# A four-layer graph network on one core: 64-wide products in pairs, a merged first message round, and a sorting network written with another instruction

## The chip, the core and the metric

The kernel runs on one core of one Trainium2 chip. The metric is device time in microseconds (us) for one execution, over all 16 batches; the median of three runs before the change is 3176.69 us (3176.14 to 3177.83). A profiled execution, from which every duration below is read, is a separate run with the profiler on.

A core has five engines with a queue each, which they work through in order: PE (TensorE, matmuls), DVE (VectorE), ACT (ScalarE), POOL (GpSimd; here it only issues gathers) and SP (SyncE, which issues DMAs). ACT and POOL issue DMAs too.

## The reference

`x` is 16 x 1024 x 64, `adj` 16 x 1024 x 1024 with about 17 nonzero entries per row, the diagonal among them. Four layers, each ending in a layernorm over the 64 channels:

```python
# layer 0
x = layernorm(x + adj @ (x @ W0) + b0)
# layer 1: quantiles over the kept neighbours of each node
adj_ = where(eye, 1, adj);  nb = (adj_ > 0) & ~eye;  m = nb.sum(-1)
rank = cumsum(nb, -1) - 1
skip = where(m > 10, (m + 1) // 2, 1)
removed = nb & (skip > 1)[..., None] & ((rank + 1) % skip[..., None] == 0)
adj_d = where(removed | removed.T, 0, adj_)
sv = sort over the kept neighbours' rows of x, channel by channel
agg = 0.25*q(0.25) + 0.5*q(0.5) + 0.25*q(0.75)      # interpolated from sv
x = layernorm(x + (relu((x + agg) @ W1 + b1) @ W2 + b2) * nodemask)
# layer 2: h = x @ We, then three message rounds
for i in range(3):
    h = relu(adj @ (h @ Wl[i] + bl[i]))
x = layernorm(x + (h @ Wp + bp) * nodemask)
# layer 3
t = adj @ x
x = layernorm(x + where(t > 0.5, 1, 0))
```

## The kernel before

**Tiles.** A batch's 1024 nodes are eight tiles (`T` = 8) of 128 (`P`); C = 64 channels, H = 128 hidden, R = 66 the pitch of a gathered row, `HALF` = 512 nodes, `NH` = 2 halves, `TH` = 4 tiles in a half. PE writes into PSUM banks of 128 partitions by 512 floats. "Node form" has nodes on the partitions, "channel form" has channels there.

**Stages of a batch.** Each is a Python generator that issues a few instructions and yields their planned length.

- `words_of` loads 128 rows of the adjacency at a time (SP, 512 KB), transposes them on PE (L439), copies them on ACT (L441), compares with zero on DVE (`nb`, L526 and L527), packs the neighbour bits into words by matmuls (L536), and feeds layer 0: `Layer0.feed` (L459 to L468) makes eight products of 64 output rows for each tile (L464). `Layer0.end` transposes `x` into the lower 64 partitions of `ax` (L478), so that one product with `w0_sb` (128 x 64, the weight above a centred identity) adds the node itself.
- `front` and `listing` work out which neighbours stay and list them (DVE: MAX8 at L707, `scalar_tensor_tensor` at L694 and L710, permutation at L646) and write a table of `x` to DRAM.
- `gathered` has POOL fetch one listed neighbour's row for each of the 128 nodes of a tile per indirect DMA (L815): 129 of them per batch. They land in the tile `g` (tag "x", four buffers).
- `masked` marks the end of each list (DVE L862, ACT L868).
- `quantiles` sorts the gathered rows: a network of minima and maxima on DVE, all at L906, 228 `tensor_tensor` instructions per batch, 3648 in all. Each takes two boxes of SBUF and writes a third, `count` by `run` slots of 64 columns; `box` builds them with a stride of 66. Neighbouring instructions depend on each other often.
- `summed` weighs the sorted rows (ACT L932) and adds them up on PE (L936).
- `back` takes the sums back to node order (`to_nodes`, one-hot matmuls at L979, closing products at L985), then w1 (L1172), residual (L1141, L1147) and layernorm; layer 2: `to_channels` (transposes L367, copies L369), We (L1185), and three rounds of message (bias L324, weight L1196, copy L1199) and product with the adjacency (L1207, relu L1210), then a residual; layer 3: `aggregate` (L372 to L381, products at L377), transposes at L1219, threshold L1222, layernorm, store.

**What is 64 wide.** The products of `feed` (L464), `aggregate` (L377), `to_nodes` (L979, L985) and the transposes of `to_channels` have 64 output rows; they fill partitions 0 to 63 of a bank, one bank for each half of the nodes, and one ACT copy of 64 x 512 for each bank. Channel-form tiles (`chan`) are 64 x 1024.

**Order.** All batches are recorded in one order, worked out in Python ahead of time: a heap of generators by planned time (L1233 to L1271). `LENGTHS` are the planned lengths of the five sort groups of a batch (192.06 us together); `WORDS`, `LISTS` and `BACK` (152.6, 133.2 and 178 us) are how long the other stages should last, and each is spread over that time by the factor `WORDS / WORDS_STEPS` and so on, where the `_STEPS` are what a stage's own yields add up to. What is recorded is what each engine's queue runs, in that order. So stages of neighbouring batches share the engines: while batch b is sorted, POOL gathers for a later group, the rows of batch b+1 are read and packed, and the back of batch b-1 runs. For batch 0's head there is nothing to sort yet; behind the last sort only the last batch's back is left. A spare branch behind it (`general`, which shares `feed`, `to_channels` and `back`) handles batches whose lists overflow; no instruction of it is in the trace.

Of the kernel before, what the change touches and what calls it, by code (L numbers as in the profile page):

```python
# [53 lines left out]
WORDS_STEPS, LISTS_STEPS, BACK_STEPS = 82.0, 74.0, 181.0  # L54
# [94 lines left out]
def network(n):  # L149
    return [tuple(map(int, op.split(","))) for op in NETS[n].split(";")]  # L150


@with_exitstack
def kernel(
# [126 lines left out]
    nc.scalar.dma_start(w0_sb[:C, :], w0)  # L281
    nc.vector.tensor_copy(w0_sb[C:, :], ident[C:, C:])
    w1_sb = load("w1_sb", [C, H], w1)
    b1_sb = load("b1_sb", [H, 1], b1.unsqueeze(1))
    w2_sb = load("w2_sb", [H, C], w2)
    we_sb = load("we_sb", [C, H], we)
# [11 lines left out]
    for v, n in ((w0_sb, 2 * C), (w2_sb, H), (wp_sb, H)):  # L298
        centred(v, n)
# [21 lines left out]

    def add_bias(bank, first, n, times):

        nc.tensor.matmul(bank[:, :times * n], ones16,  # L324
                         bias16[:, first:first + n].unsqueeze(1).to_broadcast([S, times, n]),
                         start=True, stop=False)
# [4 lines left out]
    mask_f = const.tile([B * T, P], F32, name="mask_f")  # L331
# [10 lines left out]
    def psum_mm():  # L342
        return psum("mm", 2)
# [17 lines left out]

    def to_channels(dst, src):

        for h in range(NH):
            pt = psum_mm()
            for i in range(TH):
                nc.tensor.transpose(pt[:C, i * P:(i + 1) * P], src[:, h * TH + i, :], ident)  # L367
            yield 1.5
            nc.scalar.copy(dst[:, h * HALF:(h + 1) * HALF], pt[:C, :])  # L369
            yield 1.0  # L370

    def aggregate(dst, adjT, src, bank):  # L372

        for h in range(NH):
            pa = bank()
            for m in range(T):
                nc.tensor.matmul(pa[:C, :], src[:, m, :], adjT[:, h * TH:(h + 1) * TH, m, :],  # L377
                                 start=(m == 0), stop=(m == T - 1))
                yield 1.3
            nc.scalar.copy(dst[:, h * HALF:(h + 1) * HALF], pa[:C, :])  # L380
            yield 0.7  # L381
# [38 lines left out]
    def load_x(b):  # L420
        xt = act.tile([P, T + 1, C], F32, tag="x", name="xt")
        nc.vector.memset(xt[:, 0, :], 0.0)
        nc.sync.dma_start(xt[:, 1:, :], one(x, b).rearrange("o (t p) c -> p (o t) c", p=P))
        return xt
# [27 lines left out]
    class Layer0:  # L452
# [6 lines left out]
        def feed(self, t, at):  # L459
            if t % TH == 0:  # L460
                self.bank = psum_ax()
            cols = slice((t % TH) * P, (t % TH + 1) * P)
            for m in range(T):
                nc.tensor.matmul(self.bank[:C, cols], self.xt[:, m + 1, :], at[:, m, :],  # L464
                                 start=(m == 0), stop=(m == T - 1))
            yield 2.4
            if t % TH == TH - 1:
                h = t // TH  # L468
                nc.scalar.copy(self.ax[:C, h * HALF:(h + 1) * HALF], self.bank[:C, :])
                yield 0.7  # L470

        def end(self, y):
            for h in range(NH):
                pt = psum_tp()
                for i in range(TH):

                    two = self.xt[:, h * TH + i:h * TH + i + 2, :].rearrange("p t c -> p (t c)")
                    nc.tensor.transpose(pt[:, i * P:(i + 1) * P], two, ident)  # L478
                yield 1.0
                nc.scalar.copy(self.ax[C:, h * HALF:(h + 1) * HALF], pt[C:, :])  # L480
                yield 0.7
            pz = psum_ax()
            add_bias(pz, 0, C, T)
            for t in range(T):
                nc.tensor.matmul(pz[:, t * C:(t + 1) * C], self.ax[:, t * P:(t + 1) * P], w0_sb,
                                 start=False, stop=(t == T - 1))
                if t % 2:
                    yield 0.7
            yield 1.0
            yield from layernorm(nodes(pz), y, "0")  # L490
# [400 lines left out]
    def quantiles(st, g):  # L891
        tiles, n, lo, kw = group(g)
        nt = len(tiles)
        while ("hat", g) not in st:
            yield 0.5
        bufs = st["g", g], srt.tile([P, KMAX * R], F32, tag="y", name="s", bufs=2)

        def box(buf, first, run, step, count):
            v = buf[:, first * nt * R:]
            dims = [[step * nt * R, count]] if count > 1 else []  # L900
            dims += [[R, run * nt]] if run * nt > 1 else []
            return bass.AP(tensor=v.tensor, offset=v.offset,
                           ap=[list(v.ap[0])] + dims + [[1, C]])

        for mode, a, b, d, run, sa, sb, sd, count in network(n):
            nc.vector.tensor_tensor(box(bufs[mode >> 1 & 1], d, run, sd, count),  # L906
                                    box(bufs[mode >> 3], a, run, sa, count),
                                    box(bufs[mode >> 2 & 1], b, run, sb, count),
                                    ALU.max if mode & 1 else ALU.min)
            yield (nt * count * run * C + 151) / 960  # L910
        w = tmp.tile([P, nt, kw], F32, tag="w", name="w")
        nc.vector.tensor_reduce(w, st["hat", g].rearrange("p t s k -> p t k s"), AX.X, ALU.add)  # L912
        yield 0.2
        st["sorted", g] = bufs, w
# [40 lines left out]
    def to_nodes(dst, st):  # L955
# [11 lines left out]
        banks = [psum_mm() for _ in range(NH)]  # L967
        for s in range(T):
# [8 lines left out]
            for h, bank in enumerate(banks):  # L977
                for i in range(S):
                    nc.tensor.matmul(bank[:C, :], pieces[:, i, s, :],  # L979
# [3 lines left out]
        for h, bank in enumerate(banks):  # L983
            for i in range(TH):
                nc.tensor.matmul(bank[:C, i * P:(i + 1) * P], st["x1"][:, h * TH + i, :], ident,  # L985
                                 start=False, stop=(i == TH - 1))
            yield 1.2
            nc.scalar.copy(dst[:, h * HALF:(h + 1) * HALF], bank[:C, :])
# [31 lines left out]
    def general(b):  # L1020
# [47 lines left out]
        xT = act.tile([C, N], F32, tag="chan", name="x1T")  # L1068
        run(to_channels(xT, st["x1"]))
        xrow = dram.tile([C, N], F32, tag="xrow", name="xrow", bufs=1)  # L1070
        nc.sync.dma_start(xrow, xT)
# [50 lines left out]
    def back(st):  # L1122
# [33 lines left out]
        def chan(name):  # L1156
            return act.tile([C, N], F32, tag="chan", name=name)
# [11 lines left out]
        for h in range(NH):  # L1169
            cols = slice(h * HALF, (h + 1) * HALF)  # L1170
            ph = psum_mm()
            nc.tensor.matmul(ph, w1_sb, oT[:, cols], start=True, stop=True)  # L1172
# [6 lines left out]
        x2T = chan("x2T")  # L1179
        yield from to_channels(x2T, x2)  # L1180
        hT = act.tile([H, N], F32, tag="hT", name="h0T")
        for h in range(NH):
            cols = slice(h * HALF, (h + 1) * HALF)
            ph = psum_mm()
            nc.tensor.matmul(ph, we_sb, x2T[:, cols], start=True, stop=True)  # L1185
            yield 1.3
            nc.scalar.copy(hT[:, cols], ph)
            yield 0.7
        for l in range(NL):
# [26 lines left out]
        yield from aggregate(tT, adjT, x3, psum_mm)  # L1216
        pt = psum_mm()
        for t in range(T):
            nc.tensor.transpose(pt[:, t * C:(t + 1) * C], tT[:, t * P:(t + 1) * P], ident[:C, :C])  # L1219
# [96 lines left out]
```

## Time and profile before

| | |
|---|---|
| median of three runs | 3176.69 us |
| span of the profiled execution | 4328.2 us |
| granted TensorE clock, mean | 0.764 of full speed |
| first gather starts | 96.0 us |
| sort instructions (L906) | 266.8 us to 4195.2 us, 3648 of them, 1974.6 us busy |
| last instruction ends | 4328.2 us |
| gathers (L815) | 2064, 2158.4 us busy |

The profiled execution is 1151.5 us longer than the median of the runs. Its time goes in periods of some 251 us, one for each batch, and a stretch of each has nearly idle engines. A group's "busy" is the sum of its instructions' durations; "idle before" is how long its engine stood before them, with what released it. A window's row gives, for each engine, busy time and the number of instructions, then the granted clock.

### The profile page before, as it was taken

To read this page: it belongs to the slowest core of one execution; us is meant where nothing else is said; L and a number is where in the kernel's file an instruction comes from. 1 tells how busy PE (TensorE), PEld (TensorE's weight loads), DVE (VectorE), ACT (ScalarE), POOL (GpSimd) and SP (SyncE) were. 2 spreads that over 40 slices of the span, in tenths; PEclk is the share of its full clock that TensorE was granted. 3 is DMA by queue.
4 is the path that set the end of the run, shared out by engine and by line. 5 is a ranking of instruction groups with operands and counts; after the bars stand their busy time and mean duration, and the time that the engine had idled before them with its cause. 6 is when DMAs were issued, how large, how long until landed. Compare 5 with 4: busy or idle time off the path is not lost.

```text
span 4328.2 us, 46055 instructions
## 1 busy us (share of the span) xinstructions
PE 2647.8 (61%) x13765; PEld 1635.7 (38%) x13766; DVE 2822.0 (65%) x6935; ACT 1914.0 (44%) x6153; POOL 2160.8 (50%) x2078
## 2 busy tenths in 40 slices
PE   6034285675848567584755758476575848456478
PEld 5023152443525244352533435253343525233243
DVE  6058383865849486594857668485766859476671
ACT  2034352634536264453535455363545536253641
POOL 1715626455454645546465464546545554645600
PEclk8566597787969778796877879687787969768688
DMA  3212121322222132222213222231322222111210
GB/s 107 42 50 70 34 67 37 104 54 78 73 71 84 40 101 56 78 77 74 77 39 90 64 83 76 65 84 40 100 60 79 78 80 71 39 57 24 62 43 3
DMA packets 169056, 282.54 MB, mean 65 GB/s; under 512 B 99485, under 2 KB 102112, under 8 KB 166880
## 3 DMA queue, kind: packets, MB, share of 16 engines
q1 hardware_dynamic: 67584, 142.01, 9.9%
q0 software_dynamic: 66048, 69.88, 9.1%
q10 hardware_dynamic: 35168, 67.62, 4.1%
q8 instruction: 114, 1.87, 0.2%
q14 instruction: 142, 1.16, 0.1%
HBM read 204.33 MB, written 71.44 MB: 64 GB/s over the span
## 4 chain that ended last, share of the span: by engine, by line
another core or an unknown queue 28%; DVE 25%; PE 23%; ACT 16%; issue 7%; DMA 0%; ACTq 0%; DVEq 0%
DVE g L906 7%; PE mm L1207 7%; DVE s L906 7%; ACT g L868 6%; ACT ones_at L974 3%; PE ax L464 3%; ACT ones_at L975 2%; PE tp L439 2%; PE mm L377 2%; PE pa L936 2%; PE mm L1196 2%; ACT g L932 1%; PE mm L1141 1%; DVE top L707 1%
## 5 line engine op out<-in xcount | busy, mean ns | idle before, releaser
L815 POOL DMA_INDIRECT g<-table,idx x1952 | 2045.4, 1048 | 1919.7 <-PE pa L936 666.8
L1207 PE MATMUL mm<-adjB,msg 128*128 128x512 f32 x1536 | 769.6, 621 | 109.1 <-issue 82.4
L936 PE MATMUL pa<-g,ident 128*128 128x128 f32 (+1 forms) x1600 | 376.0, 360 | 430.1 <-ACT g L932 300.5
L868 ACT ACTIVATE g<-g,bias 128x64 f32<-128x64 f32 (+9 forms) x2272 | 596.8, 341 | 47.9 <-DVE bias L864 29.2
L906 DVE TENSOR_TENSOR s<-g 128x256 f32<-128x256 f32 (+9 forms) x944 | 531.3, 588 | 64.5 <-ACT g L868 55.5
L936 PEld LDWEIGHTS pa<-g,ident 128*128 128x128 f32 x1600 | 312.3, 248 | 574.0 <-ACT g L932 347.1
L906 DVE TENSOR_TENSOR g<-s 128x256 f32<-128x256 f32 (+8 forms) x864 | 473.4, 573 | 9.0 <-DVE s L906 3.0
L932 ACT ACTIVATE g<-g,w 128x64 f32<-128x64 f32 x1552 | 397.8, 341 | 17.2 <-DVE w L912 13.6
L1207 PEld LDWEIGHTS mm<-adjB,msg 128*128 128x128 f32 x1536 | 268.7, 197 | 301.1 <-issue 270.7
L1147 DVE TENSOR_TENSOR u<-mm,mb 128x512 f32<-128x512 f32 x32 | 22.1, 691 | 463.1 <-remote 313.5
L464 PE MATMUL ax<-at,xt 128*64 128x128 f32 x1920 | 284.5, 310 | 17.4 <-issue 17.4
L377 PE MATMUL mm<-adjB,x 128*64 128x512 f32 x512 | 272.6, 666 | 36.3 <-issue 31.3
L979 PE MATMUL mm<-ones_at,pieces 128*64 128x512 bf16 x768 | 213.0, 420 | 119.0 <-ACT ones_at L975 77.1
L464 PEld LDWEIGHTS ax<-at,xt 128*64 128x64 f32 x1920 | 250.2, 158 | 81.2 <-issue 79.1
L439 PE MATMUL tp<-ident,arow 128*128 128x128 f32 x1024 | 181.7, 309 | 156.2 <-remote 66.4
L399 DVE TENSOR_REDUCE ln_v<-sq 128x8 f32<-128x512 f32 x64 | 43.6, 681 | 296.4 <-issue 156.8
L439 PEld LDWEIGHTS tp<-ident,arow 128*128 128x128 f32 x1024 | 140.9, 162 | 205.1 <-issue 131.7
L441 ACT COPY at<-tp 128x512 f32<-128x512 f32 x240 | 139.0, 580 | 177.2 <-remote 122.3
L906 DVE TENSOR_TENSOR g<-g,s 128x256 f32<-128x256 f32 (+5 forms) x432 | 199.1, 464 | 15.1 <-remote 5.0
L906 DVE TENSOR_TENSOR g<-g 128x256 f32<-128x256 f32 (+8 forms) x304 | 200.7, 660 | 11.2 <-remote 4.0
L1219 PE MATMUL mm<-ident,tT 64*128 64x64 f32 x128 | 25.7, 295 | 293.9 <-ACT tT L380 207.4
L1210 ACT ACTIVATE hlT<-mm 128x512 f32<-128x512 f32 x96 | 57.4, 598 | 296.4 <-PE mm L1207 123.7
(225 smaller groups left out, 4361.9 us busy)
## 6 DMA issues: line engine op xcount, KB each, us to landing
arow<-in_adj_dram SPq DMA_DIRECT2D x128, 512.0 KB
adjd<-at ACTq DMA_DIRECT2D x120, 512.0 KB
adjB<-adjd SPq DMA_DIRECT2D x15, 4096.0 KB
g<-table,idx POOLq DMA_INDIRECT x1952
table<-xc ACTq DMA_DIRECT2D x16, 264.0 KB
xt<-in_x_dram SPq DMA_DIRECT2D x16, 256.0 KB
out_dram<-y SPq DMA_DIRECT2D x16, 256.0 KB
stage<-table,packed POOLq DMA_INDIRECT x112
```

What stands on the lines that cost most here:

```text
L377: nc.tensor.matmul(pa[:C, :], src[:, m, :], adjT[:, h * TH:(h + 1) * TH, m, :], start=(m == 0), stop=(m == T - 1))
L439: nc.tensor.transpose(pt[:, i * P:(i + 1) * P], a[:, j * P:(j + 1) * P], ident)
L441: nc.scalar.copy(at[:, h * TH:(h + 1) * TH, :], pt.rearrange("p (i n) -> p i n", n=P))
L464: nc.tensor.matmul(self.bank[:C, cols], self.xt[:, m + 1, :], at[:, m, :], start=(m == 0), stop=(m == T - 1))
L815: nc.gpsimd.indirect_dma_start(out=dst, out_offset=None, in_=st["table"], in_offset=bass.IndirectOffsetOnAxis(ap=index, axis=0))
L868: nc.scalar.activation(v, v, AF.Identity, bias=bias[:m, i, k:k + 1])
L906: nc.vector.tensor_tensor(box(bufs[mode >> 1 & 1], d, run, sd, count), box(bufs[mode >> 3], a, run, sa, count), box(bufs[mode >> 2 & 1], b ...
L932: nc.scalar.activation(slots(g, bufs[0], lo + r, lo + r + 1)[:, i, 0, :C], slots(g, bufs[at[r]], lo + r, lo + r + 1)[:, i, 0, :C], AF.Iden ...
L936: nc.tensor.matmul(pa[:, :(e - k) * nt * C], ident, rows_.rearrange("p (k c) -> p k c", c=R)[:, :, :C], start=(j == 0), stop=(j == len(run ...
L974: nc.scalar.activation(ones_at, iota, AF.Abs, bias=st["minus"][:, s:s + 1])
L979: nc.tensor.matmul(bank[:C, :], pieces[:, i, s, :], ones_at[:, h * HALF:(h + 1) * HALF], start=(s == 0 and i == 0), stop=False)
L1207: nc.tensor.matmul(pg, msg[:, m, :], adjT[:, h * TH:(h + 1) * TH, m, :], start=(m == 0), stop=(m == T - 1))
```

## The change

It has four parts.

1. **Pairs.** `rows_of(bank, h)` is partitions 0 to 63 or 64 to 127 of a bank. `feed`, `aggregate`, `to_nodes` and `to_channels` write two products of 64 rows into the two halves of one bank, in turn, and ACT copies one 128 x 512 block where it copied two of 64 x 512. In `feed` the even neighbour tiles go to one half and the odd to the other, and the product with `w0_sb` (now the weight twice, one above the other) adds the halves; the node itself comes by a product of its own (`xT`, `self_sb`), eight more small matmuls per batch. Channel-form tiles are 128 x 512. The transposes of `to_channels` become matmuls with the identity, those at the end of layer 3 go from eight of 64 rows to four of 128, those of `Layer0.end` from eight to four.
2. **The merged first round.** Layer 2's embedding and first message weight become one 64 x 128 weight `wel_sb`, worked out once at the start: We, less its mean over the 64 inputs, times Wl[0], plus bl[0]/64 in every row. As `x2` comes out of a layernorm and so sums to zero over the channels, the product of `x2 + 1` with it equals the message with its bias. So the first round is: add one to `x2` (ACT), one paired `aggregate`, two products with `wel_sb`, relu. `to_channels(x2)`, the two products with We, two biases, 16 instructions of L1196 and one of the three rounds of L1207 are gone.
3. **Minimum and maximum.** `tensor_tensor(min or max)` becomes `scalar_tensor_tensor` (times 1.0, then min or max). Its boxes have at most two free dimensions, so where a box has more than one run, `widths` lets it run over all 66 columns of a slot.
4. **Counts.** `WORDS_STEPS` goes from 82 to 74 and `BACK_STEPS` from 181 to 149; the planned lengths of the stages stay.

```diff
-WORDS_STEPS, LISTS_STEPS, BACK_STEPS = 82.0, 74.0, 181.0
+WORDS_STEPS, LISTS_STEPS, BACK_STEPS = 74.0, 74.0, 149.0
...
+def widths(n, nt, narrow, full):
...
+    read, found = set(), []
+    for mode, a, b, d, run, sa, sb, sd, count in reversed(network(n)):
+        out = places(mode >> 1 & 1, d, run, sd, count)
+        wide = bool(out & read) or (count > 1 and run * nt > 1)
+        read -= out
+        if wide:
+            read |= places(mode >> 3, a, run, sa, count) | places(mode >> 2 & 1, b, run, sb, count)
+        found.append(full if wide else narrow)
+    return found[::-1]
...
+    weT = act.tile([H, C], F32, tag="x3", name="weT")
+    pe = ps.tile([P, HALF], F32, tag="mm", name="pe", bufs=2)
+    nc.tensor.transpose(pe[:, :C], we_sb, ident[:C, :C])
+    nc.vector.tensor_copy(weT, pe[:, :C])
+    centred(weT, H)
...
+    for h in range(2):
+        half = slice(h * C, (h + 1) * C)
+        nc.tensor.matmul(pe[half, :H], share16[:, half], bias16[:, 3 * C:3 * C + H],
+                         start=True, stop=False)
+        nc.tensor.matmul(pe[half, :H], weT, wl_sb[:, 0, :], start=False, stop=True)
+    nc.vector.tensor_copy(wel_sb, pe[:, :H])
...
+    def rows_of(t, h):
+        return t[h * C:(h + 1) * C]
+
     def to_channels(dst, src):
...
+        pt = psum_mm()
+        for i in range(TH):
+            for h in range(NH):
+                nc.tensor.matmul(rows_of(pt, h)[:, i * P:(i + 1) * P], src[:, h * TH + i, :], ident,
+                                 start=True, stop=True)
+        yield 1.5
+        nc.scalar.copy(dst, pt)
+        yield 1.0
+
+    def aggregate(dst, adjT, src, bank, tiles):
+
+        pa = bank()
+        for m in range(T):
+            for h in range(NH):
+                nc.tensor.matmul(rows_of(pa, h), src[:, m, :], adjT[:, tiles[h], m, :],
                                  start=(m == 0), stop=(m == T - 1))
-                yield 1.3
-            nc.scalar.copy(dst[:, h * HALF:(h + 1) * HALF], pa[:C, :])
-            yield 0.7
+            yield 1.3
+        nc.scalar.copy(dst, pa)
+        yield 0.7
...
             for m in range(T):
-                nc.tensor.matmul(self.bank[:C, cols], self.xt[:, m + 1, :], at[:, m, :],
-                                 start=(m == 0), stop=(m == T - 1))
-            yield 2.4
+                nc.tensor.matmul(rows_of(self.bank, m % 2)[:, cols], self.xt[:, m, :], at[:, m, :],
+                                 start=(m < 2), stop=(m >= T - 2))
+            yield 1.6
...
+                nc.tensor.matmul(pzt, self.ax[:, t * P:(t + 1) * P], w0_sb, start=False, stop=False)
+                nc.tensor.matmul(pzt, xT[:, t // 2 * P:(t // 2 + 1) * P], self_sb[:, t % 2],
                                  start=False, stop=(t == T - 1))
...
-        for mode, a, b, d, run, sa, sb, sd, count in network(n):
-            nc.vector.tensor_tensor(box(bufs[mode >> 1 & 1], d, run, sd, count),
-                                    box(bufs[mode >> 3], a, run, sa, count),
-                                    box(bufs[mode >> 2 & 1], b, run, sb, count),
-                                    ALU.max if mode & 1 else ALU.min)
-            yield (nt * count * run * C + 151) / 960
...
+        for (mode, a, b, d, run, sa, sb, sd, count), width in zip(network(n), widths(n, nt, C, R)):
+            nc.vector.scalar_tensor_tensor(box(bufs[mode >> 1 & 1], d, run, sd, count, width),
+                                           box(bufs[mode >> 3], a, run, sa, count, width), 1.0,
+                                           box(bufs[mode >> 2 & 1], b, run, sb, count, width),
+                                           op0=ALU.mult, op1=ALU.max if mode & 1 else ALU.min)
+            yield (nt * count * run * width + 151) / 960
...
             yield 1.9
-            for h, bank in enumerate(banks):
-                for i in range(S):
-                    nc.tensor.matmul(bank[:C, :], pieces[:, i, s, :],
+            for i in range(S):
+                for h in range(NH):
+                    nc.tensor.matmul(rows_of(bank, h), pieces[:, i, s, :],
                                      ones_at[:, h * HALF:(h + 1) * HALF],
                                      start=(s == 0 and i == 0), stop=False)
...
-        x2T = chan("x2T")
-        yield from to_channels(x2T, x2)
+        x2p = act.tile([P, T, C], F32, tag="msg", name="x2p")
+        nc.scalar.activation(x2p, x2, AF.Identity, bias=ones)
+        yield 1.0
+        gT = chan("gT")
+        yield from aggregate(gT, adjT, x2p, psum_mm,
+                             [slice(h * TH, (h + 1) * TH) for h in range(NH)])
         hT = act.tile([H, N], F32, tag="hT", name="h0T")
         for h in range(NH):
-            cols = slice(h * HALF, (h + 1) * HALF)
             ph = psum_mm()
-            nc.tensor.matmul(ph, we_sb, x2T[:, cols], start=True, stop=True)
+            nc.tensor.matmul(ph, rows_of(wel_sb, h), rows_of(gT, h), start=True, stop=True)
             yield 1.3
-            nc.scalar.copy(hT[:, cols], ph)
+            nc.scalar.activation(hT[:, h * HALF:(h + 1) * HALF], ph, AF.Relu)
             yield 0.7
-        for l in range(NL):
+        for l in range(1, NL):
...
-        yield from aggregate(tT, adjT, x3, psum_mm)
+        yield from aggregate(tT, adjT, x3, psum_mm, [slice(h, T, NH) for h in range(NH)])
         pt = psum_mm()
-        for t in range(T):
-            nc.tensor.transpose(pt[:, t * C:(t + 1) * C], tT[:, t * P:(t + 1) * P], ident[:C, :C])
+        for i in range(TH):
+            nc.tensor.transpose(pt[:, i * P:(i + 1) * P], tT[:, i * P:(i + 1) * P], ident)
```

## The prediction

> **What bounds the kernel now.** I read the page's top and its chain of waits first.
>
> ```profile
> span 4328.2 us, 46055 instructions
> ...
> PE 2647.8 (61%) x13765; PEld 1635.7 (38%) x13766; DVE 2822.0 (65%) x6935; ACT 1914.0 (44%) x6153; POOL 2160.8 (50%) x2078
> ...
> another core or an unknown queue 28%; DVE 25%; PE 23%; ACT 16%; issue 7%; DMA 0%; ACTq 0%; DVEq 0%
> ```
>
> No engine is full, and 28% of the chain, 1212 us, has no releaser in the trace. The span lies 1151 us above the runs' median of 3176.7, so nearly all of this belongs to the profiled execution alone: without the 1212 us it would last 3116, 2% under the median. Where that time sits, the windows show (columns: length; busy us and instructions of PE, PEld, DVE, ACT, POOL; granted clock; DMA share; GB/s):
>
> ```profile
> 2140.00:2150.00 10.00, 10.00 (x67) 6.53 (x67) 9.66 (x29) 5.70 (x19) 0.00 (x0) 1.00 0.30 107
> 2160.00:2170.00 10.00, 10.00 (x59) 6.39 (x58) 9.79 (x23) 5.98 (x20) 7.87 (x8) 1.00 0.20 38
> 2200.00:2210.00 10.00, 0.00 (x0) 0.00 (x0) 0.00 (x0) 1.58 (x8) 7.57 (x8) 0.50 0.16 27
> ```
>
> In the third only gathers run; such stretches are the profiler's. In the others DVE is busy 9.7 of 10 us. PE shows 10.00, but its ends are modelled: 2647.8 us at the mean clock of 0.764 is 2023 at full clock, 126 per batch of 181. So in the steady part DVE sets the end. Between the first sort (266.8) and the last (ends 4195.2) its instructions and the gaps under 1 us between them take 2727.3 + 105.7 = 2833 us, 177.1 per batch. The head up to the first sort is 147 us without the profiler's share: the first gather starts at 96.0, the 24 of the first group take 1.35 each, landing and masking the rest. The tail behind the last sort is 133 us and holds no gather. 147 + 2833 + 133 = 3113; the median is 64 more, 4.0 us of DVE waiting per batch. Waits of DVE in one period:
>
> ```profile
> DVE u L1147 <- remote: 32.4, 1, 32.4
> ...
> DVE u L1147 <- PE mm L1141: 6.1, 1, 6.1
> DVE cand L694 <- ACT hat L887: 2.1, 1, 2.1
> DVE s L906 <- ACT g L868: 2.1, 1, 2.1
> ```
>
> The first is the profiler's; the others, 10.3 together, are of the size wanted.
>
> **POOL is nearly level with DVE.** A gather's length depends on what DVE does (start, length, engine; the DVE row is from the same moment):
>
> ```profile
> 2101.28 1.15 POOL L815 DMA_INDIRECT g<-table,idx  x1 [0.30 <-issue]
> ...
> 2107.74 0.94 POOL L815 DMA_INDIRECT g<-table,idx  x1 [0.30 <-issue]
> ```
>
> ```profile
> 2108.20 0.55 DVE L710 SCALAR_TENSOR_TENSOR kw<-kw,top 128x320 f32<-128x320 f32 x1
> ```
>
> Sorting all 2064 gathers by the DVE operation that overlaps them most: idle DVE 946 ns (751 gathers), `tensor_tensor` of L906 1118 (998), `scalar_tensor_tensor` of L710 946 (81) and, with two whole tensors, of L694 947 by its median (10, mean 1060), reduction of L399 945 (13). Beside a DVE over 90% busy the mean is 1110. With 0.302 to the next, 2064 x 1.41 = 2914 us; plus 97 before the first gather and 212 behind the last, 3223, already above 3177. So POOL has no room, and data for the sorts can be late.
>
> **Part 3, the sorting instructions.** Price of one:
>
> ```profile
> L1147 DVE TENSOR_TENSOR u<-mm,mb 128x512 f32<-128x512 f32 x32 | 22.1, 691 | 463.1 <-remote 313.5
> ```
>
> ```profile
> L1222 DVE SCALAR_TENSOR_TENSOR u<-mm,x x16: 680/692/692, 767.3 to 4316.6; 128x512 f32<-128x512 f32 x16
> ```
>
> (The second row has minimum, median, maximum.) 512 elements cost 691 ns by the one and 692 by the other; I take no difference. Upper bound: 320 elements in L710 take 552 against 486 for a sum of that size, but that form reads a scalar per partition, ours a constant; for 8 elements the gap to a dependent instruction is 193 against 187, so 6 ns on 3648 is 22 us. Lower bound zero: no row shows it cheaper. Wider boxes: summing `count` x `run` x tiles x width over the networks of a batch, 84,736 elements become 87,314, 2,578 more; at the 0.96 per ns that L906 keeps (256: 0.42 us, 512: 0.69), 2.69 us per batch, 43 us in all. The recorded order has 82 more sort instructions waiting for the one before; after a sort instruction the next one starts 0.187 us past its elements' time when it waits for it and 0.069 when it doesn't, so each costs 0.118: 10 us. DVE sum: +53 (to +75), all on the bound engine, hidden by nothing.
>
> What it gives: with L906 acting like L694 and L710, a slot of POOL goes from 1.41 to 1.26 us, 2064 x 0.15 = 310 us of room; POOL needs 97 + 2600 + 212 = 2909 and no longer meets DVE. I let the waits fall from 4.0 to 1.0 us per batch: -48 us; bounds 0 and -64. One quarter stays because L1147 waits for PE and L694 for ACT, whatever POOL does.
>
> A rule speaks against this: the Trainium skill ("SBUF — State Buffer", Who interferes with whom) says that a DVE instruction with two SBUF inputs contends with a GpSimd instruction that reads SBUF. By it both forms, with two tensors in SBUF, would hold the gathers up alike, and the relief would be nothing. L694 has two SBUF tensors as well, and the median of its gathers, 947 ns, speaks against the rule for this form; ten are few.
>
> **Part 1, pairs.** At full clock a product of 512 columns in float32 is two instructions of 0.43 us, 128 or 64 wide alike. No row shows two 64-wide products on the two halves of a bank, so one pair costs between one product (side by side) and two (one after the other). Per batch, side by side saves 6.9 in `aggregate` (32 x 0.43 = 13.8 halved), 7 in `feed` (13.9), 5 in `to_nodes` (48 instructions x 0.22), and with part 2 the replacement of a round of 13.8 by 6.9 and the lost L1185, L1196 and L367: 29 us in all; one after the other 3.5. In the steady part either lies under DVE (126 of 181 us), and counts only as an earlier L1147. Eight small products more in layer 0 (0.1 each) are as covered. ACT loses 4.6 us per batch, of 1914 / 16 = 120, also covered. The bare stretch is the tail:
>
> ```profile
> 4243.57 15.17 PE L1207 MATMUL mm<-adjB,msg 128*128 128x512 f32 x32
> ```
>
> ```profile
> 4298.87 16.55 PE L377 MATMUL mm<-adjB,x 128*64 128x512 f32 x32 [4.79 <-DVE x L411]
> ```
>
> The stretch from x2 to the first hidden state, 4233.0 to 4259.4, is 26.4 us; a paired aggregate of 7.6 to 8.3, two copies and two products make 12 to 14: -13. L377 halves: -8. The 15.2 us of to-nodes (PE there 13.1, ACT between): -4; copies and closing products: -2. Sum -27 side by side; one after the other -8, since only the We, message and copy steps go. The halves write different partitions and depend on nothing of each other, so I take side by side.
>
> **Part 2** adds set-up. In the recorded order all of DVE's constants, with the copies of weT and `wel_sb` that wait for PE, now stand ahead of batch 0's first `nb`, which started at 14.09; behind it wait the bits, the lists and the first gather: +4 to +7. Feeding batch 0 (64.4 - 49.28 = 15 us of PE for its eight tiles) halves, some of it on that path: -3. The 24 first gathers at 0.15 less could give -4, but sorts don't run there yet, so nothing. Head +2 (-4 to +7).
>
> No DMA is added where the kernel runs: SP's order grows by one, the store at L1071 in the spare branch, which the trace shows not taken; POOL's stays as it is. The steps keep their places in SP's and POOL's order. Nothing for that.
>
> **Part 4** issues nothing. Fewer steps over the same 178 us stretch each, so L1147's first instance comes some 8 us of plan later; its row waits 6.1 for PE, and later placement can only shorten that. If instead the back ran late, the next adjB load behind it would: bounds 0 and +1 per batch, inside the 4.0.
>
> **Sum:** 147 + 2 head, 2833 + 53 steady, 133 - 27 tail, 16 waits: 3157. Against 3176.7: +2 +53 -27 -48 = -20.
>
> **Rivals.**
>
> *The boxes cost more than POOL gives (ends slower).* Place: L906 on DVE. The waits belong to PE and ACT (L1147, L694, L868 rows above), or the relief fails as by the rule; then they stay 4.0. 3176.7 + 2 + 53 - 27 = 3205. It decides where less than (53 + 2 - 27) / 16 = 1.75 us of wait per batch goes away. For it: all DVE waits in that period name PE or ACT, none a gather. Against: 3223 of POOL demand.
>
> *POOL was the only bound.* Then all 64 go, and the first gathers gain 4: 3177 + 2 + 53 - 27 - 64 - 4 = 3137; should part of the 105.7 us of small gaps also be late data (a quarter, say), 3111. For it: 3223 against DVE's 3113. Against: DVE 9.7 of 10.
>
> *Pairs run one after the other.* Tail -8: 3157 + 19 = 3176, no change. For it: nothing in the trace has such a pair. Against: nothing either.
>
> **How the numbers follow.** Forecast 0.44, slower rival 0.24, POOL alone 0.18, serial pairs 0.14. A measurement of this kernel tells 0.2% from no change: 3170.3 to 3183.0. Faster: 0.38 of the forecast, all 0.18, 0.03 of the serial case: 0.59. Same: 0.05 + 0.07 = 0.12. Slower: 0.01 + 0.04 + 0.24 = 0.29. The forecast's own range, from bounds on waits (8 to 32) and dependent gaps (0 to 10), is 3139 to 3173. The whole range reaches to the slower rival and to POOL alone with its gaps: 3110 to 3206; beyond lie the 22 us of instruction price above 3205, and the part below 3110.
>
> **What would show it.** Gathers with a mean near 0.96 us where they now have 1.05; sort instructions adding up to about 2020 us (1975 now) with the same duration for the same size; in the paired `aggregate` two instructions started within 0.43 us, the group in the tail near 8 us; tail near 106; first `nb` some 4 to 7 later. Wrong if gathers stay at 1.12 beside the sorts, if starts in a pair keep 0.43 apart, or if a 512-element sort instruction takes over 0.70.

## The result, and the profile after

The changed kernel takes 3388.57 us (3387.05 to 3394.25, four runs) against 3176.41 (3174.85 to 3177.83): a ratio of 1.067, 95% interval 1.0655 to 1.0686. It is 212 us slower, where 20 faster had been forecast.

One thing has to be known for the numbers: on some chips the kernel before takes 3175 to 3177 us, on others 4341 to 4489, with PE standing still for tens of us in each batch (why is open); the profile of before shown above is of the second kind, the result and the profile of this section are of the first.

The page of the changed kernel, its busy line and its chain:

```profile
span 3385.3 us, 45329 instructions
...
PE 2360.3 (70%) x13484; PEld 1435.8 (42%) x13485; DVE 2885.3 (85%) x6933; ACT 1854.9 (55%) x6041; POOL 2277.1 (67%) x2078
...
DVE 36%; POOL 35%; issue 12%; PE 8%; DMA 5%; ACT 3%; DVEq 0%; POOLq 0%; ACTq 0%
...
L857 POOL DMA_INDIRECT g<-table,idx x1952 | 2154.5, 1104 | 924.1 <-issue 573.0
```

The part without a releaser is gone from the chain: DVE and POOL hold it in turn, so this span can be read as it stands. DVE is busy 63 us longer than before (2822.0), of which the wider boxes were to make 43. A gather takes 1104 ns in the mean, not 960. Now DVE's waits, for the whole run (engine, line, releaser: us in total, times, longest):

```profile
DVE ag L996 <- ACT half L995: 105.0, 17, 11.6
DVE u L1196 <- PE mm L1190: 85.4, 17, 48.8
DVE ln_v L441 <- ACT sq L438: 63.6, 15, 5.2
DVE ln_r L447 <- ACT ln_sd L444: 42.6, 17, 3.4
```

These waits come once in nearly every batch; the 48.8 of the second row lies in the tail. Cut as the prediction's sum was cut, the span is: head 143.2 (to the first sort), instructions and gaps under 1 us of DVE from the first to the last sort 2788.0 + 91.3 = 2879.3, waits over 1 us in that stretch 254.3, tail 108.6; together 3385.4. The forecast had 149, 2886, 16 and 106. Three terms are right within 7 us. The waits are 254 instead of 16, and that is the whole miss: `ag` L996 makes 102 of them, `ln_v` L441 61, `ln_r` L447 39, `u` L1196 29, and `hits` L904, which waits for gathers, 22.

The tail shows the pairs (PE, start, length, then what stood before):

```profile
3310.34 10.00 PE L419 MATMUL mm<-adjB,x2p 128*64 128x512 f32 x32 [5.54 <-ACT x2p L1229]
...
3363.07 9.24 PE L419 MATMUL mm<-adjB,x 128*64 128x512 f32 x32 [4.79 <-DVE x L453]
```

32 instructions take 9.24 us where the same 32 took 16.55 (each group in part at a granted clock of 0.50); the two of a pair start 0.00 to 0.01 us apart, pairs 0.43 apart once the granted clock is 1.0.

### The profile page after: what moved, and what is told of

The parts are those of the page before. It is cut to its first block, busy times and chain, and to the rows that moved or that the text cites. A ratio compares the mean times of both kernels' runs of the same rounds, so it can differ in the third digit from the quotient of the medians.

```text
span 3385.3 us, 45329 instructions
## 1 busy us (share of the span) xinstructions
PE 2360.3 (70%) x13484; PEld 1435.8 (42%) x13485; DVE 2885.3 (85%) x6933; ACT 1854.9 (55%) x6041; POOL 2277.1 (67%) x2078
## 4 chain that ended last, share of the span: by engine, by line
DVE 36%; POOL 35%; issue 12%; PE 8%; DMA 5%; ACT 3%; DVEq 0%; POOLq 0%; ACTq 0%
POOL g L857 33%; DVE g L953 11%; DVE s L953 11%; DMA g<-table,idx 4%; DVE top L749 3%; POOL stage L857 2%; DVE kw L752 2%; PE mm L1259 2%; PE mm L419 2%; DVE nb L568 1%; PE pa L983 1%; ACT ones_at L1021 1%; ACT g L979 1%; ACT g L910 1%; ACT ones_at L1022 1%
## 5 line engine op out<-in xcount | busy, mean ns | idle before, releaser
L857 POOL DMA_INDIRECT g<-table,idx x1952 | 2154.5, 1104 | 924.1 <-issue 573.0
L953 DVE SCALAR_TENSOR_TENSOR s<-g 128x264 f32<-128x264 f32 (+9 forms) x944 | 547.3, 604 | 6.9 <-DVE g L953 0.5
L1259 PE MATMUL mm<-adjB,msg 128*128 128x512 f32 x1024 | 513.6, 623 | 4.0 <-ACT msg L1251 4.0
L953 DVE SCALAR_TENSOR_TENSOR g<-s 128x264 f32<-128x264 f32 (+10 forms) x864 | 486.7, 584 | 4.0
L979 ACT ACTIVATE g<-g,w 128x64 f32<-128x64 f32 x1552 | 394.6, 337 | 130.5 <-DVE w L959 130.5
L419 PE MATMUL mm<-adjB,x2p 128*64 128x512 f32 x512 | 153.7, 739 | 110.6 <-ACT x2p L1229 110.6
L953 DVE SCALAR_TENSOR_TENSOR g<-g,s 128x264 f32<-128x264 f32 (+6 forms) x432 | 204.2, 475 | 7.3
L953 DVE SCALAR_TENSOR_TENSOR g<-g 128x264 f32<-128x264 f32 (+8 forms) x304 | 204.8, 674 | 5.8
L928 ACT ACTIVATE hat<-iota,npos 128x10 f32<-128x10 f16 (+2 forms) x384 | 114.4, 298 | 160.0 <-DVE npos L917 153.5
L693 PE MATMUL wd<-hi,perm 128*128 128x71 f16 x960 | 115.8, 238 | 113.5 <-DVE perm L688 110.6
L953 DVE SCALAR_TENSOR_TENSOR s<-s,g 128x264 f32<-128x264 f32 (+4 forms) x400 | 149.5, 380 | 5.7
L505 PE MATMUL ax<-at,xt 128*64 128x128 f32 x1920 | 153.9, 311 | 0.7 <-DVE xc L453 0.7
```

What stands on the lines that cost most here:

```text
L419: nc.tensor.matmul(rows_of(pa, h), src[:, m, :], adjT[:, tiles[h], m, :], start=(m == 0), stop=(m == T - 1))
L505: nc.tensor.matmul(rows_of(self.bank, m % 2)[:, cols], self.xt[:, m, :], at[:, m, :], start=(m < 2), stop=(m >= T - 2))
L693: nc.tensor.matmul(pw[:, :hn], ws, hi[:, t, :], start=False, stop=False)
L857: nc.gpsimd.indirect_dma_start(out=dst, out_offset=None, in_=st["table"], in_offset=bass.IndirectOffsetOnAxis(ap=index, axis=0))
L953: nc.vector.scalar_tensor_tensor(box(bufs[mode >> 1 & 1], d, run, sd, count, width), box(bufs[mode >> 3], a, run, sa, count, width), 1.0, ...
L979: nc.scalar.activation(slots(g, bufs[0], lo + r, lo + r + 1)[:, i, 0, :C], slots(g, bufs[at[r]], lo + r, lo + r + 1)[:, i, 0, :C], AF.Iden ...
```

## The experiments

Lines of the changed sources differ from kernel to kernel; tiles and operations keep their names. "Ratio" is to the kernel before in the same comparison.

### Was the long profile of before an accident? (e1, e7)

No edit: first the kernel before, then the changed one, profiled again.

> The kernel before, unchanged, profiled once more, because its first profiled execution lasted 4328 us against 3176 in the runs. If the stretches with nearly idle engines were an accident of that one profile, this span is near 3180, the gathers have a mean of 1.09 to 1.15 us, and waits of DVE between the first and the last sort come to about 64 us in all, as the prediction had it. If they belong to this kernel under the profiler, the span is again over 4000 and the granted clock of the quiet stretches again 0.50.

4304 us, 4299 to 4383 in seven runs beside it. The quiet stretches are there again, and they lengthen runs, not only one profile: the prediction's "such stretches are the profiler's" was wrong. They seem to belong to the chip: every run of one comparison is of one kind, and a chip that was used twice was of the same kind both times; what on the chip makes them isn't shown. Comparisons on such chips answer another question than the 3176 to 3389, and of what follows only the runs beside a kernel before of 3175 to 3177 are used for the cause.

> The changed kernel, unchanged, beside the kernel before. On a chip where the kernel before takes 3176: 3388 again, whatever theory. On one where it takes 4350 (in the four trials so far PE stood still for tens of us in each batch there), the theory that the loss is in DVE's waits for PE's slow stretches expects them to be hidden behind those standstills, ratio 1.00 to 1.03; the theory that it is in the sorts' form expects a ratio of 1.03 or more.

3388.03 us, ratio 1.0677 (1.0659 to 1.0695): the result stands in a second comparison.

### The sorts' form alone (e2, e5, e9)

The kernel before with part 3 and `widths`, nothing else:

```diff
-            nc.vector.tensor_tensor(box(bufs[mode >> 1 & 1], d, run, sd, count),
...
+            nc.vector.scalar_tensor_tensor(box(bufs[mode >> 1 & 1], d, run, sd, count, width),
```

> The kernel before with part 3 alone (scalar_tensor_tensor, boxes of 64 or 66 columns). The theory that the sorts' new form is the loss (wider boxes, gathers held up as before) expects most of the 212 us here: 3330 to 3400. The theory that the loss comes from PE (pairs and merged round leave it idle more often, its granted clock falls to 0.50, and DVE waits in order for slow products) expects only the DVE price of 53, with waits unchanged: 3215 to 3240. The prediction's own sum, with gathers set free, would be 3180.

> The kernel before with part 3 alone, once more, because in the first trial of it even the kernel before took 4341 us instead of 3176. Judged by the ratio to the kernel before in the same comparison. Sorts' form is the loss: 1.05 to 1.07. PE's clock or the order is the loss: 1.01 to 1.02 (the DVE price of 53 us). The prediction's own sum, with gathers set free: 1.00.

> The kernel before with part 3 alone, now hoped for on a chip where the kernel before takes 3175. Sorts' form is the loss: 3330 to 3390. Order or products are the loss: 3210 to 3240 (the DVE price of 53). The prediction's sum: 3180.

The first two ran beside a kernel before of 4341 and 4356 us (ratios 1.0123 and 1.0158). The third beside 3177.05: 3224.46 us, ratio 1.0151 (1.0134 to 1.0168), +47 us. That is the DVE price, and no gather was set free. POOL's group in this kernel:

```profile
L831 POOL DMA_INDIRECT g<-table,idx x1952 | 2139.1, 1096 | 755.5 <-issue 564.1 <-DVE nb L542 92.8 <-DVE g L927 34.5
```

Sorted by the DVE operation over them, the 1439 gathers beside the new sorts have a mean of 1127 ns, those beside idle DVE 943 (63): the new form holds gathers up like the old one (1118 in the profile of before).

Means of this kind mix two things, and the traces show a sharper picture when gathers are sorted by what DVE runs at the moment they start. In e11 (below; the same sorts) 716 gathers start in the middle of a sort instruction, at least 0.08 us behind its start and over 0.15 us ahead of its end. Each lasts what is left of that instruction and then 0.82 us more (0.811 to 0.827). Under `tensor_tensor`, in the profile of before, it is the same: 501 gathers, 0.82 us in the mean. The 84 that start in the middle of a MAX8, which has one input, take 0.944 us, as with idle DVE, and so do the 13 that start under L1196, one of whose two inputs lies in PSUM. And a gather that starts within 0.03 us of an instruction's own start gets through: the 31 at the start of a `tensor_tensor` with two SBUF inputs (L743) take 0.944 as well. So for the sorts the operation makes no difference: both forms have two inputs in SBUF, and both hold a gather that starts under them until they end. (Two inputs aren't the only thing that does it: 57 gathers that start under the `tensor_scalar` at L568, which has one, also last what is left of it and 0.81 us more.)

This run is also the clean picture of the old order: DVE's waits over 1 us between first and last sort are 77 us, the head is 138.0, the tail 130.9. Of the 77, 30 are waits for gathers (`hits` L878), all of them before 308 us or after 2988; in the batches between, no wait over 1 us is for a gather.

### The sorts undone (e3, e6, e10)

The changed kernel with `tensor_tensor` and 64 columns again (the diff above, reversed).

> The changed kernel with part 3 undone (tensor_tensor, 64 columns), pairs, merged round and new step counts kept. If the sorts' form is the loss: 3150 to 3180. If PE's clock or the order is: only the 43 to 53 us of DVE come back, 3325 to 3350.

> The changed kernel with part 3 undone, once more. Sorts' form is the loss: ratio to the kernel before 0.98 to 1.00. PE's clock or the order is the loss: 1.045 to 1.055, since only the 43 to 53 us of DVE come back.

> The changed kernel with part 3 undone, on such a chip. Sorts' form is the loss: 3140 to 3180. Order or products are the loss: 3325 to 3350.

Beside 4341 and 4356 us: 4369 both times (ratio 1.0013 in the second). Beside 3177.05: 3362.20, ratio 1.0577 (1.0559 to 1.0596), 26 us under the changed kernel; DVE's busy time falls 50 us between the sorts, its waits grow from 254 to 278. So part 3 is worth 26 to 47 us of the loss. Gathers beside these `tensor_tensor` sorts: mean 1162 (1380 of them), against 1137 (1372) in the changed kernel.

### The step counts undone (e4, e11, e14)

```diff
-WORDS_STEPS, LISTS_STEPS, BACK_STEPS = 74.0, 74.0, 149.0
+WORDS_STEPS, LISTS_STEPS, BACK_STEPS = 82.0, 74.0, 181.0
```

> The changed kernel with part 4 undone (step counts 82 and 181 as before, so that the shortened stages end earlier in the plan). If the new counts put instructions of the back where DVE must wait for them, a good part of the waits (7.0 us before ag, 5.1 and 3.4 in a layernorm, each period) goes: 3200 to 3300. If PE's clock or the sorts' form is the loss: 3370 to 3410.

> The changed kernel with the step counts of before, on such a chip. If the new counts place instructions where DVE waits in order (7.0 us before ag and so on): 3200 to 3300. If the sorts' form is the loss: 3370 to 3410.

Beside 4341 us: 4448 (1.027). Beside 3177.05: 3269.75, ratio 1.0292 (1.0275 to 1.0309). Two constants, which add no instruction and take none away, make 119 of the 212 us. DVE's waits between the sorts fall from 254 to 125, and in one period (201 us of the changed kernel, then 191 of this one) they read:

```profile
DVE ag L996 <- ACT half L995: 7.0, 1, 7.0
DVE ln_v L441 <- ACT sq L438: 5.2, 1, 5.2
DVE ln_r L447 <- ACT ln_sd L444: 3.4, 1, 3.4
DVE u L1196 <- PE mm L1190: 1.3, 1, 1.3
```

```profile
DVE ln_v L441 <- ACT sq L438: 4.1, 1, 4.1
DVE cand L736 <- ACT wd L730: 1.9, 1, 1.9
DVE u L1196 <- PE mm L1190: 1.0, 1, 1.0
DVE ag L996 <- ACT half L995: 0.2, 1, 0.2
```

Where the 7.0 us come from, PE's order shows. In the changed kernel, with the new counts, around one such wait (DVE stood from 1780.7 to 1787.7):

```profile
1773.83 0.80 PE L983 MATMUL pa<-g,ident 128*128 128x128 f32 x2 [2.75 <-ACT g L979]
1774.55 2.07 PE L1221 MATMUL mm<-oT,w_sb 64*128 64x512 f32 x2
1776.56 1.22 PE L983 MATMUL pa<-g,ident 128*128 128x128 f32 x4
1778.36 0.80 PE L983 MATMUL pa<-g,ident 128*128 128x128 f32 x2 [0.58 <-ACT g L979]
1779.09 2.07 PE L1221 MATMUL mm<-oT,w_sb 64*128 64x512 f32 x2
```

and ACT at the same time:

```profile
1776.66 0.69 ACT L1223 ACTIVATE hT<-mm,b_sb 128x512 f32<-128x512 f32 x1 [1.93 <-PE mm L1221]
...
1781.20 0.69 ACT L1223 ACTIVATE hT<-mm,b_sb 128x512 f32<-128x512 f32 x1 [1.94 <-PE mm L1221]
```

The weighted sum of a sorted group is a chain from DVE (`w`) over ACT (L979) and PE (`pa`) back to DVE (`ag`). The back's two products with w1 (L1221), 2.07 us each at a clock of 0.50, now stand inside it: ACT waits for each (1.93, 1.94) with the scalings of the chain queued behind. From `w` to `ag` it takes 14.74 us, and DVE has 8.0 us of other work recorded in between. With the old counts the back comes at another place: 10.61 us, 11.3 us of other work, no wait (e9: 10.84 and 11.5). The plan knows nothing of this: it gives each stage a start and a pace.

> The changed kernel with the step count of the back alone set back to 181, that of the words left at 74. If the back's stretched steps are what DVE waits for (ag, the residual and the layernorms of the back): nearly all of the 118 us, 3265 to 3300. If the words' count matters as much: 3320 to 3350.

Beside 4437 us: 4649, ratio 1.0484 (1.0405 to 1.0563). On that kind of chip this isn't comparable, so which of the two counts does it is open.

### More work for PE (e8)

```diff
-            for m in range(T):
+            for m in [*range(T), *range(T)]:
                 nc.tensor.matmul(rows_of(self.bank, m % 2)[:, cols], self.xt[:, m, :], at[:, m, :],
...
-        for m in range(T):
+        for m in range(2 * T):
             for h in range(NH):
-                nc.tensor.matmul(rows_of(pa, h), src[:, m, :], adjT[:, tiles[h], m, :],
-                                 start=(m == 0), stop=(m == T - 1))
-            yield 1.3
+                nc.tensor.matmul(rows_of(pa, h), src[:, m % T, :], adjT[:, tiles[h], m % T, :],
+                                 start=(m % T == 0), stop=(m % T == T - 1))
+            yield 0.65
```

> The changed kernel with the products of feed and of both aggregates issued twice (the first set is written over by the second), which puts back some 21 us of PE work per batch and changes nothing else. If PE's idle time and the clock of 0.50 that follows it are the loss, the granted clock rises and the time falls: 3250 to 3350 where the changed kernel takes 3388. If the sorts' form or the order is the loss: 3388 to 3430.

The mean clock rises to 0.795 (0.733), but the time to 3445.76 (ratio 1.0858, 1.0839 to 1.0876), and the waits to 301 us; neither theory had expected more than 3430. More work for PE is no remedy: even with a better clock it made the chains longer, not shorter. What the clock costs by itself this run can't say, since the doubled products lie in the same chains (the tail alone grows from 108.6 to 120.3 us).

### What is left: the products (e12, e13, e16, e17, e15)

With the old counts and the new sorts in both, the products are the difference of 3269.75 (e11) and 3224.46 (e9): 45 us, with 48 more of DVE's waits, a tail 22 us shorter (109.0 against 130.9) and a head 6.6 longer (144.6 against 138.0). The windows of one period each (length; busy us and instructions of PE, PEld, DVE, ACT, POOL; granted clock), e9 and then e11:

```profile
1295.00:1482.00 187.00, 153.50 (x864) 93.21 (x864) 178.26 (x427) 119.49 (x389) 140.84 (x130) 0.92 0.32 97
```

```profile
1271.70:1462.90 191.20, 135.18 (x844) 85.22 (x844) 178.38 (x426) 116.01 (x378) 142.19 (x130) 0.77 0.32 95
```

PE has less to do, DVE the same, and the granted clock falls from 0.92 to 0.77. The new wait is at layer 0's end. There, PE in e9 and then in e11:

```profile
1244.39 0.38 PE L340 MATMUL ax<-bias,ones 3*128 3x512 bf16 x1
1244.70 1.10 PE L501 MATMUL ax<-w_sb,ax 128*128 128x64 f32 x8
...
1248.33 0.66 PE L501 MATMUL ax<-w_sb,ax 128*128 128x64 f32 x4
```

```profile
1455.86 0.80 PE L983 MATMUL pa<-g,ident 128*128 128x128 f32 x2 [7.26 <-ACT g L979]
1456.59 0.60 PE L362 MATMUL ax<-bias,ones 3*128 3x512 bf16 x1
1457.12 0.69 PE L526 MATMUL ax<-w_sb,ax 128*128 128x64 f32 x2
1457.61 0.63 PE L527 MATMUL ax<-self_sb,xT 128*128 128x64 f32 x2
```

In e9, 16 instructions at a clock of 1.0 take 4.64 us from the bias to the square on ACT, and no wait follows on DVE. In e11 there are 32 (each `w_sb` with its `self_sb`), at 0.50, PE having idled 7.26 us just before; they take 9.79 us, and DVE waits 4.1 for it. Between the first and the last sort there are 14 such waits, 60 us together, more than the whole difference. With the new counts it is 13.96, as the pairs of the last `aggregate` stand between. To see it by taking it away, layer 0 alone was put back:

```diff
-                nc.tensor.matmul(rows_of(self.bank, m % 2)[:, cols], self.xt[:, m, :], at[:, m, :],
-                                 start=(m < 2), stop=(m >= T - 2))
-            yield 1.6
+                nc.tensor.matmul(self.bank[:C, cols], self.xt[:, m + 1, :], at[:, m, :],
+                                 start=(m == 0), stop=(m == T - 1))
+            yield 2.4
...
-                nc.tensor.matmul(pzt, xT[:, t // 2 * P:(t // 2 + 1) * P], self_sb[:, t % 2],
```

> The changed kernel with parts 3 and 4 both undone: what is left is the products (pairs and merged round). If the three losses add up (part 4 118 us, part 3 26 to 47): 3223 to 3244. If with the old order the sorts' form costs nothing, or pays: 3260 or more. If the products alone were a gain, as the prediction had it: under 3177.

> As e12, and layer 0 with single 64-wide products and the order of the words as in the kernel before; only the back keeps pairs and merged round. If the shorter feed and the longer chain of small products at layer 0's end make DVE wait (4.1 us before ln_v in each batch): 3160 to 3200. If the loss sits in the back: as e12.

> The changed kernel with the step counts of before and layer 0 as before (single 64-wide products, eight transposes, no extra products for the node itself); sorts, back and merged round stay changed. Between the kernel before with part 3 alone (3224) and the changed kernel with the old step counts (3270) lie the products, 45 us. If layer 0's shorter feed and its longer closing chain are that loss: 3200 to 3235, and the 4.1 us of waiting before ln_v in each batch goes. If it is the back's pairs and merged round: 3255 to 3275. PE's share of half clock, 23% in the one and 47% in the other, tells how far it goes with PE's work.

> As e16, once more, because there even the kernel before took 4489 us. Ratio to the kernel before where that takes 3177: layer 0 is the loss 1.007 to 1.018, the back is the loss 1.025 to 1.030.

All four ran beside a kernel before of 4356 to 4489 us: e12 1.0246 (1.016 to 1.0332), e13 1.0112 (1.0036 to 1.0187), e16 1.043, e17 1.0384 (1.0344 to 1.0424). Layer 0 put back looks better with the old sorts (e13 against e12) and, with the new ones, has no partner on such a chip but e4 (1.027, against which it looks worse). So how the 45 us divide between layer 0 and the back stays open; the wait at layer 0 is seen in the trace, not taken away.

e15 put 12 products into one idle stretch of PE (written over afterwards):

```diff
+        for _ in range(12):
+            nc.tensor.matmul(pa, ident, ident, start=True, stop=True)
         step = 2 // nt
```

> As e12, with 12 products of 128 x 128 put into PE's queue ahead of each weighted sum, where PE stood idle up to 7 us (2.6 us of work at full clock, five times per batch; their result is written over). If the granted clock of 0.50 after idle stretches lengthens the chains that DVE waits for: 10 to 40 us faster than e12, share of half clock well down. If the clock doesn't matter: 0 to 40 us slower than e12.

1.0413 (1.0327 to 1.05) beside 4437 us: 95 us slower than e12 there, more than either theory had expected, and for the second time no gain from a busier PE. On the other kind of chip it was not tried.

### The products where nothing lies over them (e18)

The kernel before, with the new aggregate and merged round in the last batch's back only:

```diff
+        last = st["b"] == B - 1 if isinstance(st["b"], int) else False
+        if last:
+            x2p = act.tile([P, T, C], F32, tag="msg", name="x2p")
...
+            yield from paired(gT, adjT, x2p, [slice(h * TH, (h + 1) * TH) for h in range(NH)])
...
+    add(100.0, merged())
```

> The kernel before, with the paired aggregates and the merged first round in the back of the last batch alone, and the merged weight worked out once during the first batch's sorts; every other batch, the sorts and the order stay as before. If the tail behind the last sort is the one place where the products pay (109 us in the changed kernel, 131 in the kernel before with part 3 alone), and to-nodes and w1 there stay as they were: 15 to 22 us under the kernel before, 3155 to 3162 where that takes 3177. If the tail's shortening came from elsewhere, or the extra set-up costs more than 10 us: 3175 to 3190.

Beside 4481.94 us it took 4463.89, ratio 0.9966 (0.9927 to 1.0005): 18 us less, not clear of that chip's spread. Its tail, which holds no gather, is 112.0 us against 131.4 in e1. That it would beat 3176 is therefore likely and not shown.

## Why the prediction was wrong, step by step

- **What bounds the kernel.** Held for DVE: its work between first and last sort was forecast at 2886 and is 2879. The quiet stretches, "the profiler's" in the prediction, lengthen runs too; that didn't harm the sum, which left them out.
- **Part 3, price.** Held: +53 forecast, +47 measured alone (e9). The sort instructions are 42 us longer in all (2017.0 against 1974.6), the 43 of the wider boxes; no price per instruction showed beyond that.
- **Part 3, what it gives: the step that failed first.** "With L906 acting like L694 and L710": those two hold gathers up as well. L710 has two tensor inputs in SBUF (the same tile, `cur`, twice); in e11 (there L752) the 34 gathers that start in the middle of it last what is left of it and 0.82 us more (0.812 to 0.821), exactly as under a sort. The prediction sorted gathers by the operation that lies over them longest, and of some 80 that fell to L710 so, 54 had started under the MAX8 ahead of it and were through. Its own rows show it, with the DVE rows that run when the two gathers start:

```profile
2101.06 0.55 DVE L710 SCALAR_TENSOR_TENSOR kw<-cand,top 128x320 f32<-128x320 f32 x1
...
2107.67 0.49 DVE L707 MAX8 top<-kw 128x8 f32<-128x320 f32 x1
```

  The gather of 1.15 us starts at 2101.28, with 0.33 us of L710 left (0.33 + 0.82 = 1.15); the one of 0.94 starts at 2107.74 under MAX8, and L710 begins only at 2108.20. L694's ten gathers had a mean of 1060, and I took the median of 947: six of the ten had started beside idle DVE. In the changed kernel 63 gathers lie beside that line: mean 1268. The Trainium skill ("SBUF — State Buffer", Who interferes with whom) said so: two SBUF inputs contend with a reading GpSimd, whatever the operation. The measurement sides with the rule. Nor was there much to relieve: in e9 DVE waits 30 us for gathers, in the first and the last batch only, where the prediction had 48 to win in all batches.
- **Waits fall from 4.0 to 1.0 us per batch: the term that decided.** They rose to 15.9 (254 / 16), all but 22 us of it behind PE and ACT. With the old counts and products (e9) they are 77 in all, near the 64 of the prediction's sum, as the slower rival had it.
- **Part 4, "later placement can only shorten": wrong, and the largest piece,** 119 us. I costed one instruction's wait (L1147) and took the rest of the order as free. The paces of the back and of the words decide what stands inside the other stages' chains: DVE's waits fall from 254 to 125 us with the old counts.
- **Eight small products more "as covered".** They lie in a chain to DVE: 4.64 us became 9.79 (e11, at half the clock) and 13.96 (changed kernel), with a wait of 4 to 5 us in most batches.
- **PE's relief counts "only as an earlier L1147".** Less work also went with a lower clock, 0.77 (e11) or 0.73 (changed kernel) instead of 0.92 (e9) in a period, and so with slower products where a chain needs them. How much of the 45 us, or of the 119, that makes by itself is open; e8 shows that more work is no remedy.
- **Pairs side by side, tail -27:** held; a tail of 106 forecast, 108.6 measured, 130.9 without (-22).
- **Head +2:** +5 (143.2 against 138.0 in e9), inside the bounds given.

Step by step from the kernel before, then: the sorts 47 us (e9), the products 45 (e11 against e9), the counts 119 (the changed kernel against e11). As each step starts where the last one ends, these must add up to the 212; in another order the shares differ, since undoing the sorts alone under the new counts gives back only 26.

## What to carry to other kernels

In an order written ahead of time, the lengths given to the stages are part of the kernel: when instructions are taken out, try the old pace before the recounted one, and look in the trace at what then stands inside each chain that goes from the bounding engine over others and back. An engine with time to spare wasn't free of cost here: work removed from it gained in the tail, where nothing lies over it, and work added to it cost time where a chain passes. For whether an operation holds up gathers, sort them by what runs when they start, not by what lies over them longest; and ask first whether the waits that are to go are waits for gathers at all.

## What the hardware showed beside that

PE's clock. In the changed kernel, windows of 2.5 us (length; busy us of PE with its instructions; granted clock; DMA share; GB/s):

```profile
1695.00:1697.50 2.50, 0.00 (x0) 1.00 0.15 25
1697.50:1700.00 2.50, 0.67 (x2) 0.66 0.15 26
...
1712.50:1715.00 2.50, 2.50 (x10) 0.50 0.16 30
...
1717.50:1720.00 2.50, 2.50 (x12) 0.74 0.18 27
```

Some 4 us into this idle stretch the clock drops to 0.50, and it stays there for 20 us although PE's row reads fully busy from 1700 on (its ends are modelled); it comes back about 3.7 us after 16 `aggregate` instructions start in a row at 1715.09. Small products in a mixed order, a full row notwithstanding, did not bring it back. The Trainium skill ("TensorE: Matmul & The Clock Gate", Part 1: The HAM clock gate) gives one busy window of about 3.4 us as what it takes; this agrees if such a mix doesn't count as busy.
